# Layer 0 of a Mamba hybrid: two tiles' products in one instruction, both PSUM work tiles in one, and the carried state brought in by ScalarE

## The chip, the cores and the metric

The kernel runs on one core of one Trainium2 chip. The metric is the device time of one execution in microseconds; before the change the median of three runs is 3914.21 us. The profile is of one more execution. Engines are named as the profile names them: PE (matmuls), DVE (VectorE), ACT (ScalarE), POOL (GpSimd) and SP (whose queue issues the DMAs).

## The reference

The program is a chain of four layers on a (4, 96, 64, 64) image. The change touches layer 0 alone: two Mamba blocks in a row, each with a recurrence over the 4096 pixels.

```python
def _mamba_block(seq, ...):                       # seq: (4, 4096, 96)
    h = (seq - mu) * rsqrt(var + EPS) * ln_g + ln_b
    xs, z = split(h @ in_w, 2)                    # 192 channels each
    xc = silu(conv_b + sum(conv_w[:, k] * xp[:, k:k + L, :] for k in range(4)))
    dbl = xc @ xproj_w                            # dt (6), B (16), C (16)
    delta = softplus(dt @ dt_w + dt_b)
    dA = exp(delta[..., None] * A)                # 192 channels x 16 states
    dBx = delta[..., None] * Bm[:, :, None, :] * xc[..., None]
    # h[t] = dA[t] * h[t-1] + dBx[t]
    y = einsum('blds,bls->bld', hstates, Cm) + Dp * xc
    return (y * silu(z)) @ out_w
```

The recurrence has 4 x 192 x 16 independent rows of 4096 steps in each of the two blocks.

## The kernel before

**Items and tiles.** Layer 0 (`layer0`) splits the 4096 steps into four stretches of T = 1024. An *item* is one image, one stretch and one block: 32 items. An item has 24 *tiles* of 128 rows x 1024 steps: the 192 x 16 rows are cut by channel third p (0 to 2), state group g (0 to 3, four states each) and half j (0 or 1). `order` lists them; within a third it is the list `eight`. So there are 768 tiles, and the index `t` of a tile within its item runs from 0 to 23.

**What a tile needs.** DVE runs the recurrence (`tensor_tensor_scan`, L486): the decay `da`, the input `u`, a starting value from `state` (or 0 in the first stretch), and the states `hs` as output. ACT computes `da` = exp(delta x A) (L464). The input `u` is `udb` (delta times xc, repeated over four states) times B. For 8 of the 24 tiles (`pool_tiles`) POOL multiplies it from SBUF into `up` (L470), with B repeated by DMA into `brep`. For the other 16, PE repeats B into PSUM with a selection matrix (`rep`, L450: two matmuls in the program, four in the profile) and DVE multiplies (L482). POOL multiplies every `hs` with C (`crep`, L492), in place, and PE sums over the states into `y` (L511). ACT copies the last column of `hs` into `state` (L499).

**The PSUM work tiles.** Two tiles of 128 x 1024 fp32 lie in PSUM with one buffer each: tag `x` holds `rep`, tag `u` holds either a product `u` or, for the 8 tiles of POOL, their decay, then called `dap`. A product whose next tile is one of POOL's is written in place over `rep`.

**Order.** The engines' order is written out by hand in a loop over slots `m`, one tile per slot (`tc.manual_schedule`). Slot m issues the product and scan of tile m; then `dap` or `rep` of tile m + 1 (`rep` only at `group_starts`, since tiles with the same p and g share it); then `da` of tile m + 3 (`AHEAD`); then POOL's product with C of tile m - 1, the state copy of tile m - 3, and further back the sums over states, the gate with `z` (L522), the projection and the output. The first stage of a later item (norm, convolution, `dbl`, `delta`, `z`, and the DMAs that repeat rows over the partitions) is spread over the same slots by `at_slot`, whose number minus 24 is the slot relative to the item's first tile. Waits between engines are put in by the program's builder from the tiles that an instruction reads and writes; the author writes none.

Of the kernel before, what the change touches and what calls it, by code (L numbers as in the profile page):

```python
# [50 lines left out]
class Net:  # L51
# [43 lines left out]
    def layer0(self, dram, scratch):  # L95
        tc, nc, ins = self.tc, self.nc, self.ins
        x_in = ins["x"]
        with ExitStack() as ctx:
            cp = ctx.enter_context(tc.tile_pool(name="l0c", bufs=1))
            psum = ctx.enter_context(tc.tile_pool(name="l0p", bufs=2, space=PSUM))  # L100
            psum_x = ctx.enter_context(tc.tile_pool(name="l0x", bufs=1, space=PSUM))
            psum_y = ctx.enter_context(tc.tile_pool(name="l0y", bufs=2, space=PSUM))
# [11 lines left out]
            def wide(rows, cols, k):  # L114
                return psum_x.tile([128, T], F32, name="w_ps", tag="xu"[k % 2])[:rows, :cols]
# [113 lines left out]
            def global_pool():  # L229

                for b in range(B):
                    for s in range(NSC):
                        xt = wk.tile([128, T + 1], F32, name="gp_x", tag="hs", bufs=9)[:C, :T]
                        nc.sync.dma_start(xt, x_in[b, :, s * T : (s + 1) * T])
                        k = b * NSC + s
                        nc.vector.reduce_sum(pooled[:, k : k + 1], xt, axis=mybir.AxisListType.X)
                    yield
                pool4 = cp.tile([C, B], F32, name="pool4")
                nc.vector.reduce_sum(pool4, pooled.rearrange("p (b s) -> p b s", b=B), axis=mybir.AxisListType.X)
                ps = small(C, B)  # L240
                nc.tensor.matmul(ps, gpw, pool4, start=True, stop=True)
                gp = cp.tile([C, B], F32, name="gp")
                nc.scalar.activation(gp, ps, AF.Relu, scale=1.0 / L, bias=self.v("gp_b"))
                yield
                ps = small(C, B)
                nc.tensor.matmul(ps, fus[:, 1, :], gp, start=True, stop=True)
                nc.scalar.activation(fbias, ps, AF.Identity, bias=self.v("fus_b"))
                yield
# [6 lines left out]
            def first_stage(k):  # L255
# [11 lines left out]
                @at_slot(-11)  # L267
                def _():
                    m["xn"] = load_x(b, s, i) if k else x0


                @at_slot(-6)
                def _():
                    m["ps"] = [tile_ps(128), tile_ps(128)]
                    for q in range(8):
                        nc.tensor.matmul(
                            m["ps"][q // 4][:, q % 4 * C : q % 4 * C + C],
                            m["xn"][:, q * 128 : q * 128 + 128],
                            self.center,
                            start=True,  # L280
                            stop=True,
                        )

                @at_slot(-5)
                def _():
                    m["nt"] = cp.tile([128, 8, C], F32, name="nt", tag="nt")
# [11 lines left out]
                @at_slot(-4)  # L298
# [5 lines left out]
                @at_slot(-3)  # L304
# [7 lines left out]
                @at_slot(-2)  # L312
# [23 lines left out]
                parts_of("xc", [(w_x[:, i, k], k) for k in range(4)], n, ((-1, 1), (0, 2), (2, 4)), 2)  # L336

                @at_slot(4)
                def _():
                    nc.scalar.activation(m["xc"], m["xc"], AF.Silu)  # L340
                    exp_set()

# [3 lines left out]
                @at_slot(7)  # L346
# [4 lines left out]
                @at_slot(8)  # L351
# [6 lines left out]
                parts_of("delta", [(dtw[:, i], 0)], dbl, ((9, 10), (9, 10), (10, 11)), 1)  # L358

                @at_slot(11)  # L360
                def _():
                    nc.scalar.activation(m["delta"], m["delta"], AF.Softplus)  # L362
                    exp_set()

                parts_of("z", [(w_z[:, i], 3)], n, ((11, 12), (12, 13), (13, 14)), 3)

                @at_slot(12)
                def _():
                    m["dd"] = dram.tile([DIN, T], F32, name="dd", tag="dd", bufs=2)
                    for at, rows in both:  # L370
                        nc.sync.dma_start(m["dd"].rearrange("(p c) t -> c p t", p=3)[:, :, at], m["delta"][rows])

                def du(p):
                    if p == 0:
                        m["ud"] = dram.tile([DIN, T], F32, name="ud", tag="ud", bufs=2)
                    of = slice(p, p + 1)
                    u = wk.tile([128, 1, MB], F32, name="du", tag="du")
                    nc.gpsimd.tensor_mul(u, m["delta"][:, of], m["xc"][:, of])  # L378
                    to = m["ud"].rearrange("(p c) t -> c p t", p=3)[:, of]
                    for at, rows in both:  # L380
                        nc.sync.dma_start(to[:, :, at], u[rows])

                for p in range(3):
                    at_slot(14 + 3 * p)(lambda p=p: du(p))

                @at_slot(16)
                def _():
                    nc.scalar.activation(m["z"], m["z"], AF.Silu)
                    exp_set()


                for p in range(3):
                    for j in range(2):
                        at_slot((16, 24, 32)[p] + j)(lambda p=p, j=j: load_d(m, "dd", p, j))
                        at_slot((18, 26, 34)[p] + j)(lambda p=p, j=j: load_d(m, "ud", p, j))
                for g, t in ((0, 10), (1, 21), (3, 23), (2, 25)):
                    at_slot(t)(lambda g=g: load_c(m, g))
                at_slot(19)(lambda: load_b(m, 3))
                at_slot(15)(lambda: load_b(m, 2))
                return steps  # L400

# [9 lines left out]
            def load_c(made, g):  # L411
                made["crep", g] = load_s(made, "crep", NST + 4 * g, 5)
# [4 lines left out]
            def load_d(made, k, p, j):  # L417

                t = wk.tile([128, T], F32, name=f"{k}b", tag=f"{k}b", bufs=4)
                row = 64 * p + 32 * j  # L420
                for s4 in range(4):
                    nc.sync.dma_start(t[32 * s4 : 32 * s4 + 32], made[k][row : row + 32])
                made[k, p, j] = t
# [5 lines left out]
            eight = [(0, 0), (0, 1), (3, 0), (1, 1), (1, 0), (3, 1), (2, 0), (2, 1)]  # L429
            order = [(p, g, j) for p in range(3) for g, j in eight]  # L430
            pool_tiles = (2, 5, 7, 10, 13, 15, 18, 21)
            group_starts = (0, 3, 6, 8, 11, 14, 16, 19, 22)
            NTL = len(order)
# [9 lines left out]
            def rep(m):  # L443

                k, t = divmod(m, NTL)
                x = psum_x.tile([128, T], F32, name="rep", tag="x")
# [6 lines left out]
                return x  # L453

            def exp(m):
# [3 lines left out]
                if on_pool(m):  # L459
                    da = psum_x.tile([128, T], F32, name="dap", tag="u")  # L460
# [5 lines left out]
            def times_b(m):  # L466
                k, t = divmod(m, NTL)
                h, g, j = order[t]
                u = made[k]["u", t] = wk.tile([128, T], F32, name="up", tag="up", bufs=2)
                nc.gpsimd.tensor_mul(u, made[k]["ud", h, j], made[k]["brep", g])  # L470

            def scan(m, x):
# [4 lines left out]
                if on_pool(m):  # L477
                    u = made[k].pop(("u", t))
                else:

                    u = x if on_pool(m + 1) else psum_x.tile([128, T], F32, name="u", tag="u")
                    nc.vector.tensor_mul(u, made[k]["ud", h, j], x)  # L482
                hs = made[k]["hs", t] = wk.tile([128, T + 1], F32, name="hs", tag="hs", bufs=9)
                col = column(t)
                st = state[:, b, i, col : col + 1]
                nc.vector.tensor_tensor_scan(hs[:, 1:], made[k].pop(("da", t)), u, 0.0 if s == 0 else st, ALU.mult, ALU.add)  # L486

            def times_c(m):

                k, t = divmod(m, NTL)  # L490
                hs = made[k]["hs", t]
                nc.gpsimd.tensor_mul(hs[:, :T], hs[:, 1:], made[k]["crep", order[t][1]])  # L492

            def keep_state(m):
                k, t = divmod(m, NTL)
                b, s, i = items[k]
                col = column(t)
                if s < NSC - 1:
                    nc.scalar.copy(state[:, b, i, col : col + 1], made[k]["hs", t][:, T:])  # L499
# [5 lines left out]
            def sum_y(k, t0):  # L505

                for q, at in enumerate(halves):
                    for t in (t0, t0 + 1):
                        p, g, j = order[t]
# [4 lines left out]
                            made[k]["hs", t][:, at],  # L514
# [40 lines left out]
            b_slots = {2: 5, 4: 7, 7: 10, 9: 13, 12: 15, 15: 18, 18: 21, 23: NTL + 2}  # L555
# [3 lines left out]
            for m in sorted(stages[0])[:4]:  # L559
                for f in stages[0].pop(m):  # L560
                    f()
            prepare()
            wk = ctx.enter_context(tc.tile_pool(name="l0w", bufs=1))
            with tc.manual_schedule(engines=engines):
                gp = global_pool()
                first = min(stages[0])
                for m in range(first, last + 19):
                    k, t = divmod(m, NTL)
                    if 0 <= m < last:
                        scan(m, x)  # L570
                    if 0 <= m + 1 < last:
                        if on_pool(m + 1):
                            exp(m + 1)
                        elif (t + 1) % NTL in group_starts:
                            x = rep(m + 1)
                    if 0 <= m + AHEAD < last and not on_pool(m + AHEAD):
                        exp(m + AHEAD)
                    if 1 <= m <= last:
                        times_c(m - 1)
                    if 3 <= m < last + 3:  # L580
                        keep_state(m - 3)
                    if -1 <= m and t in b_slots and m - t + b_slots[t] < last:
                        times_b(m - t + b_slots[t])
                    for k0 in range(max(k - 1, 0), min(k + 1, len(items))):
                        at = m - NTL * k0
                        for p in range(3):
# [3 lines left out]
                            if at - 8 * p in (4, 6, 8, 10):  # L590
                                sum_y(k0, at - 4)
                            if at == 8 * p + 11:
                                gate(k0, p)
                        if at == 34:
                            made[k0]["x"] = load_x(*items[k0])
                        if at == 39:
                            project(k0)
                        if at == 41:
# [4 lines left out]
                    if m in (-20, -17, -14, -11, 15, 16):  # L603
# [878 lines left out]
```

## Time and profile before

| | |
|---|---|
| median of 3 runs | 3914.21 us (3908.41 to 3924.87) |
| the profiled execution's own time | 3925.66 us |
| its span, first to last instruction | 3923.9 us |
| mean granted PE clock | 0.855 |
| first and last scan of layer 0 start at | 77.34 and 2610.18 us |
| busy over the span | PE 82%, DVE 80%, ACT 62%, POOL 74% |
| DMA | 463.31 MB, mean 118 GB/s |

Layer 0 takes about two thirds of the span, and then come the other three layers. In the profile's groups a line reads: source line, engine, operation, output and inputs by the program's names, shapes, count; then busy time in all and mean ns of one; then the engine's idle time just before these instructions, and what ended most of it. In a timeline a line gives start and duration in us, and in square brackets the idle time before it with its releaser.

### The profile page before, as it was taken

How to read it: one execution, taken by the hardware profiler on the slowest of the kernel's cores; microseconds unless marked ns; L12 is line 12 of the kernel's file. 1: busy time of each engine (PE TensorE's matmuls, PEld its weight loads, DVE VectorE, ACT ScalarE, POOL GpSimd, SP SyncE). 2: the span in 40 equal slices, each digit the busy share in tenths (PEclk: the TensorE clock that was granted, in tenths of full speed). 3: DMA queues.
4: the chain of work that ended last, by engine and by line, in shares of the span. 5: the costliest groups of instructions: out<-in, count | busy, mean ns of one | idle time of the engine just before them, and what ended most of it. 6: DMA issues, size and time to landing. Idle time of an engine off the chain costs nothing. (4 is left out here: it accounts for less than half of the span.)

```text
span 3923.9 us, 43975 instructions
## 1 busy us (share of the span) xinstructions
PE 3205.9 (82%) x13534; PEld 1294.8 (33%) x13534; DVE 3154.4 (80%) x2772; ACT 2420.6 (62%) x4644; POOL 2911.4 (74%) x1443
## 2 busy tenths in 40 slices
PE   6887878877878788877878887755899988899988
PEld 3222222222222222222222222115644534666643
DVE  5999999999999999999999999973374385444649
ACT  4666667766766676666766666532254676666557
POOL 2999999999999999999999999961101064444427
PEclk7788878898788888888878878766899999999989
DMA  7567656675666566756676566636300000011101
GB/s 188 135 162 171 151 130 168 164 170 131 164 158 173 132 165 154 172 140 158 153 171 150 143 161 163 159 90 211 140 1 0 1 1 6 15 36 33 39 7 59
DMA packets 179828, 463.31 MB, mean 118 GB/s; under 512 B 52852, under 2 KB 54782, under 8 KB 176256
## 3 DMA queue, kind: packets, MB, share of 16 engines
q1 hardware_dynamic: 179592, 460.49, 46.7%
q8 instruction: 108, 1.77, 0.2%
q14 instruction: 128, 1.05, 0.1%
HBM read 386.81 MB, written 73.50 MB: 117 GB/s over the span
## 5 line engine op out<-in xcount | busy, mean ns | idle before, releaser
L492 POOL TENSOR_TENSOR hs<-hs,crep 128x1024 f32<-128x1024 f32 x768 | 1797.7, 2364 | 48.0 <-DVE hs L486 26.1
L450 PE MATMUL rep<-dbl,sel_b 32*128 32x512 f32 x1152 | 407.8, 785 | 495.8 <-DVE hs L486 428.3
L464 ACT ACTIVATE da<-ddb,nega 128x1024 f32<-128x1024 f32 x512 | 584.9, 1150 | 47.2 <-DVE hs L486 40.0
L470 POOL TENSOR_TENSOR up<-udb,brep 128x1024 f32<-128x1024 f32 x256 | 605.2, 2364 | 8.8 <-DMA brep<-cd 8.8
L464 ACT ACTIVATE dap<-ddb,nega 128x1024 f32<-128x1024 f32 x256 | 286.0, 1117 | 409.3 <-DVE hs L486 408.5
L511 PE MATMUL y<-hs,sel_r 128*32 128x512 f32 x3072 | 476.4, 690 | 5.5 <-POOL hs L492 5.5
L486 DVE TENSOR_TENSOR_SCAN hs<-da,state,rep 128x1024 f32<-128x1024 f32 x192 | 450.8, 2348 | 16.7
L486 DVE TENSOR_TENSOR_SCAN hs<-da,state,u 128x1024 f32<-128x1024 f32 x192 | 450.9, 2348 | 11.2 <-DVE u L482 1.4
L486 DVE TENSOR_TENSOR_SCAN hs<-dap,state,up 128x1024 f32<-128x1024 f32 x192 | 446.7, 2326 | 0.4 <-ACT dap L464 0.4
L210 PE MATMUL ps<-n,w_x 97*64 97x512 f32 x1536 | 408.0, 679 | 9.3 <-ACT n L319 6.6
L482 DVE TENSOR_TENSOR u<-udb,rep 128x1024 f32<-128x1024 f32 x256 | 314.7, 1229 | 74.4 <-PE rep L450 46.0
L450 PEld LDWEIGHTS rep<-dbl,sel_b 32*128 32x128 f32 x1152 | 107.0, 214 | 794.5 <-issue 595.7
L482 DVE TENSOR_TENSOR rep<-udb,rep 128x1024 f32<-128x1024 f32 x256 | 310.3, 1212 | 0.2
L1040 POOL CAST hq<-y 128x1536 fp8e5<-128x1536 f16 x64 | 94.0, 1469 | 219.3 <-issue 122.6
L210 PEld LDWEIGHTS ps<-n,w_x 97*64 97x64 f32 x1536 | 118.6, 153 | 295.2 <-issue 243.5
L511 PEld LDWEIGHTS y<-hs,sel_r 128*32 128x32 f32 x3072 | 65.2, 114 | 336.5 <-issue 208.5
L378 POOL TENSOR_TENSOR du<-delta,xc 128x512 f32<-128x512 f32 x96 | 122.6, 1277 | 64.7 <-ACT delta L362 50.2
L914 POOL MEMSET h<- 1x4096 f32 x1 | 3.5, 3507 | 212.8 <-DVE n L820 212.8
L1179 POOL TENSOR_TENSOR av<-av,ec 128x780 f32<-128x780 f32 x32 | 58.8, 1837 | 133.2 <-ACT av L1176 133.2
L486 DVE TENSOR_TENSOR_SCAN hs<-da,rep 128x1024 f32<-128x1024 f32 x64 | 146.5, 2289 | 5.4
L224 PE MATMUL ps<-xc,xproj 64*102 64x512 f32 x384 | 147.3, 924 | 3.5 <-ACT xc L340 3.5
L486 DVE TENSOR_TENSOR_SCAN hs<-da,u 128x1024 f32<-128x1024 f32 x64 | 146.4, 2288 | 3.7 <-DVE u L482 0.5
(262 smaller groups left out, 6137.7 us busy)
## 6 DMA issues: line engine op xcount, KB each, us to landing
ddb<-dd SPq DMA_DIRECT2D x768, 128.0 KB
udb<-ud SPq DMA_DIRECT2D x768, 128.0 KB
crep<-cd SPq DMA_DIRECT2D x512, 128.0 KB
brep<-cd SPq DMA_DIRECT2D x256, 128.0 KB
dd<-delta SPq DMA_DIRECT2D x64, 384.0 KB
ud<-du SPq DMA_DIRECT2D x192, 128.0 KB
band<-in_band SPq DMA_DIRECT2D x24, 1024.0 KB
x<-in_x SPq DMA_DIRECT2D x32, 384.0 KB
```

Of the source, the lines that this page charges most:

```text
L210: nc.tensor.matmul(ps[rows], w[:, 64 * p : 64 * p + 64], rhs[:, at.start + shift : at.stop + shift], start=k == 0, stop=k == len(ws) - 1, ...
L224: nc.tensor.matmul(ps, w[rows, p], x[rows, p], start=start and p == 0, stop=p == 2)
L378: nc.gpsimd.tensor_mul(u, m["delta"][:, of], m["xc"][:, of])
L450: nc.tensor.matmul(x[:, at], sel_b[rows, order[t][1]], made[k]["dbl"][rows, at], start=True, stop=True)
L464: nc.scalar.activation(da, made[k]["dd", h, j], AF.Exp, scale=nega[:, col : col + 1])
L470: nc.gpsimd.tensor_mul(u, made[k]["ud", h, j], made[k]["brep", g])
L482: nc.vector.tensor_mul(u, made[k]["ud", h, j], x)
L486: nc.vector.tensor_tensor_scan(hs[:, 1:], made[k].pop(("da", t)), u, 0.0 if s == 0 else st, ALU.mult, ALU.add)
L492: nc.gpsimd.tensor_mul(hs[:, :T], hs[:, 1:], made[k]["crep", order[t][1]])
L511: nc.tensor.matmul(made[k]["y", p][row : row + 32], sel_r, made[k]["hs", t][:, at], start=False, stop=True, skip_group_check=True,)
L1040: nc.gpsimd.tensor_copy(q, y2, saturate=False)
L1179: nc.gpsimd.tensor_add(v[:, 2:4], v[:, 0:2], ec)
```

## The change

One PSUM tile `pair_ps` of 128 x 2 x 1024 takes the place of tags `x` and `u`: half 1 holds what `rep` held, half 0 what `u` and `dap` held. Its halves are used by the same instructions as the two tiles were, with these differences:

- Where two neighbouring tiles with the same p and g are both DVE's (`paired`, 6 of an item), one product of 2048 columns reads half 1 twice and writes both halves; `order` has two tiles exchanged so that they are neighbours. Four products of 1024 columns stay.
- `hs` holds both j of a pair (5 buffers of 2 x 1025 in place of 9 of 1025). POOL multiplies both with C in one instruction of 2 x 1024 columns, and the state copy takes two columns. POOL's products with B of group 3 are paired too, and `du` becomes one product of 1536 columns in place over `delta`.
- For the 16 tiles of DVE the scan starts from the constant 1.0 (0.0 in the first stretch), and ACT multiplies the first column of `da` with the state (`enter`). The 8 tiles of POOL read the state as before.
- `udb` is loaded by pairs, `crep` has one buffer per group, `nt` shares a buffer with `up2`, the Silu of `z` stands behind that of `xc`, and the first stage's slots and the slots of gate, projection and output move.

The diff, cut to its core:

```diff
+            pair_ps = psum_x.tile([128, 2, T], F32, name="pair")
...
-                parts_of("xc", [(w_x[:, i, k], k) for k in range(4)], n, ((-1, 1), (0, 2), (2, 4)), 2)
+                parts_of("xc", [(w_x[:, i, k], k) for k in range(4)], n, ((-3, -1), (-2, 0), (0, 2)), 2)
...
+                    nc.gpsimd.tensor_mul(m["delta"], m["delta"], m["xc"])
+                    spread_out("delta", "ud")
...
             def load_c(made, g):
-                made["crep", g] = load_s(made, "crep", NST + 4 * g, 5)
+                made["crep", g] = load_s(made, f"crep{g}", NST + 4 * g, 1)
...
-            eight = [(0, 0), (0, 1), (3, 0), (1, 1), (1, 0), (3, 1), (2, 0), (2, 1)]
+            eight = [(0, 0), (0, 1), (3, 0), (1, 0), (1, 1), (3, 1), (2, 0), (2, 1)]
...
+            paired = (0, 3, 8, 11, 16, 19)
+            ends = {1: 0, 4: 1, 5: 3, 7: 2}
...
             def rep(m):
...
-                x = psum_x.tile([128, T], F32, name="rep", tag="x")
+                x = pair_ps[:, 1]
...
                 if on_pool(m):
-                    da = psum_x.tile([128, T], F32, name="dap", tag="u")
+                    da = pair_ps[:, 0]
...
+            def enter(m):
+                k, t = divmod(m, NTL)
+                b, s, i = items[k]
+                col = column(t)
+                if s:
+                    a0 = made[k]["da", t][:, :1]
+                    nc.scalar.mul(a0, a0, state[:, b, i, col : col + 1])
+
+            def twice(x):
+                return x[:, None, :].to_broadcast([128, 2, T])
...
                 if on_pool(m):
-                    u = made[k].pop(("u", t))
+                    u = made[k].pop(("up", h, g, j))
+                elif t in paired:
+                    u = pair_ps[:, 0]
+                    nc.vector.tensor_mul(pair_ps, made[k]["ud", h], twice(pair_ps[:, 1]))
+                elif t - 1 in paired:
+                    u = pair_ps[:, 1]
                 else:
-
-                    u = x if on_pool(m + 1) else psum_x.tile([128, T], F32, name="u", tag="u")
-                    nc.vector.tensor_mul(u, made[k]["ud", h, j], x)
-                hs = made[k]["hs", t] = wk.tile([128, T + 1], F32, name="hs", tag="hs", bufs=9)
+                    u = pair_ps[:, 1 if on_pool(m + 1) else 0]
+                    nc.vector.tensor_mul(u, made[k]["ud", h][:, j], pair_ps[:, 1])
+                if ("hs", h, g) not in made[k]:
+                    made[k]["hs", h, g] = wk.tile([128, 2, T + 1], F32, name="hs", tag="hs", bufs=5)
+                hs = made[k]["hs", h, g][:, j]
...
-                nc.vector.tensor_tensor_scan(hs[:, 1:], made[k].pop(("da", t)), u, 0.0 if s == 0 else st, ALU.mult, ALU.add)
+                nc.vector.tensor_tensor_scan(hs[:, 1:], made[k].pop(("da", t)), u, 0.0 if s == 0 else st if on_pool(m) else 1.0, ALU.mult, ALU.add)
...
+            def times_c(k, p, g):
+
+                hs = made[k]["hs", p, g]
+                nc.gpsimd.tensor_mul(hs[:, :, :T], hs[:, :, 1:], twice(made[k]["crep", g]))
```

## The prediction

> **What bounds the kernel now.** I read the page's first two parts first, then the busy time of the stretch that the change touches.
>
> ```profile
> PE 3205.9 (82%) x13534; PEld 1294.8 (33%) x13534; DVE 3154.4 (80%) x2772; ACT 2420.6 (62%) x4644; POOL 2911.4 (74%) x1443
> ...
> DVE  5999999999999999999999999973374385444649
> ...
> POOL 2999999999999999999999999961101064444427
> PEclk7788878898788888888878878766899999999989
> ```
>
> The first 26 of the 40 slices are layer 0, and there VectorE (DVE) and GpSimd (POOL) are both at nine tenths. The busy time of each engine from 75 to 2612 us says it more finely (columns: PE, PEld, DVE, ACT, POOL, granted clock, DMA share, GB/s):
>
> ```profile
> 75.00:2612.00 2537.00, 2026.70 (x8230) 582.10 (x8230) 2431.20 (x1378) 1650.79 (x3004) 2484.72 (x1122) 0.82 0.63 154
> ```
>
> POOL is busy 98% of it and DVE 96%: two engines bind together. The DVE timeline has the first scan at 77.34 us and the last at 2610.18: 2532.8 us for 767 tiles, so 79.2 us for an item of 24 tiles, 32 items in all. The groups give the durations:
>
> ```profile
> L492 POOL TENSOR_TENSOR hs<-hs,crep 128x1024 f32<-128x1024 f32 x768 | 1797.7, 2364 | 48.0 <-DVE hs L486 26.1
> L450 PE MATMUL rep<-dbl,sel_b 32*128 32x512 f32 x1152 | 407.8, 785 | 495.8 <-DVE hs L486 428.3
> ...
> L464 ACT ACTIVATE dap<-ddb,nega 128x1024 f32<-128x1024 f32 x256 | 286.0, 1117 | 409.3 <-DVE hs L486 408.5
> ...
> L486 DVE TENSOR_TENSOR_SCAN hs<-da,state,u 128x1024 f32<-128x1024 f32 x192 | 450.9, 2348 | 11.2 <-DVE u L482 1.4
> L486 DVE TENSOR_TENSOR_SCAN hs<-dap,state,up 128x1024 f32<-128x1024 f32 x192 | 446.7, 2326 | 0.4 <-ACT dap L464 0.4
> ...
> L482 DVE TENSOR_TENSOR u<-udb,rep 128x1024 f32<-128x1024 f32 x256 | 314.7, 1229 | 74.4 <-PE rep L450 46.0
> ...
> L486 DVE TENSOR_TENSOR_SCAN hs<-da,rep 128x1024 f32<-128x1024 f32 x64 | 146.5, 2289 | 5.4
> ```
>
> The last column matters most. PE and ACT wait long for scans (428 us before `rep`, 408 us before `dap`), yet DVE waits 0.4 us for `dap` and 46 us for `rep`: both are made while DVE does something else. The timeline shows with what (start, duration, idle before in brackets; DVE, then ACT, then PE):
>
> ```profile
> 1265.58 2.35 DVE L486 TENSOR_TENSOR_SCAN hs<-da,state,u 128x1024 f32<-128x1024 f32 x1
> 1267.84 1.21 DVE L482 TENSOR_TENSOR rep<-udb,rep 128x1024 f32<-128x1024 f32 x1
> 1269.15 2.35 DVE L486 TENSOR_TENSOR_SCAN hs<-da,state,rep 128x1024 f32<-128x1024 f32 x1
> 1271.41 2.33 DVE L486 TENSOR_TENSOR_SCAN hs<-dap,state,up 128x1024 f32<-128x1024 f32 x1
> 1273.94 1.23 DVE L482 TENSOR_TENSOR u<-udb,rep 128x1024 f32<-128x1024 f32 x1 [0.20 <-PE rep L450]
> ```
> ```profile
> 1267.96 1.12 ACT L464 ACTIVATE dap<-ddb,nega 128x1024 f32<-128x1024 f32 x1 [6.26 <-DVE hs L486]
> ```
> ```profile
> 1254.62 2.07 PE L450 MATMUL rep<-dbl,sel_b 32*128 32x512 f32 x4 [3.14 <-DVE hs L486]
> ...
> 1272.76 1.13 PE L450 MATMUL rep<-dbl,sel_b 32*128 32x512 f32 x4
> ```
>
> Tiles 0, 1, 2 of an item: `dap` for tile 2 starts when scan 0 has freed `u` (1267.93) and is ready at 1269.08, under product 1 and scan 1, 2.3 us before scan 2. `rep` for tile 3 lies under scan 2. That works because `rep` and `u`/`dap` are two tiles in PSUM, and each waits only for the readers of its own.
>
> [...]
>
> **The change, part by part, per item.** Start-to-start times are read off the DVE timeline.
>
> Removed from DVE: six products become halves of six others. Two now take 1.26 + 1.31. One of 2048 columns takes 1.26 and 1024 columns more, [...]1.13 by the trace (1229 less the 665 of the 512-column gate, doubled)[...]. Sixteen scans get the constant 1.0 in place of a state column, 2289 against 2348: 16 x 0.06 = 1.0 us (24 of 32 items; the others had a constant). [...] Added to ACT: 16 multiplies of one column, near the 0.19 us of a state copy, 0 to 3 us; removed: 12 state copies (2.2) and one pair of table loads (2.6). ACT is busy 1650.8/32 = 51.6 of 79 us, so either sign is hidden. Moved at no cost, with one answer: the steps of `nt`, `xc`, `dbl`, `delta` and `z`, two to four slots earlier or later, and on SP the loads (as many as before: 24 + 24 of `ddb`, `udb`, 16 + 8 of `crep`, `brep` per item; `ud` in two stores instead of six). Each keeps three slots or more before its use, and a slot grows to 4.3 us below. `crep` has one buffer per group, so its load waits for POOL's last product of that group, up to five slots before the next use. `delta` times `xc`, now in place, holds POOL until the `dd` stores have landed; the cover is POOL's slack, 75 busy of over 100 us. If that cover were gone, a landing of some us per item would be DVE's too.
>
> Moved, and this decides: both PSUM tiles are now one, `pair_ps`. In the built program each wait can be followed to the instruction that raises its semaphore. Before, `dap` of tile 2 waits for scan 0, and `rep` of tile 3 for scan 1. After, `dap` of tile 2 waits for scan **1**, and `rep` of tile 3 for scan **2**, although they touch the other half: a write waits for the last reader of any part of the tile. All eight `dap` and all nine `rep` of an item wait this way for the scan just ahead of their user on DVE. So nothing covers them:
>
> - `dap`: 0.03 (scan end to ACT start, in 132 cases) + 1.12 + 0.10 (132.82 to 132.92, one of DVE's four waits for it) = 1.24 us, with a ready ACT. x8 = 9.9. Bounds 1.2 to 1.5. Behind it on ACT wait `da` and the state copies, three tiles ahead, so not urgent.
> - `rep`: 0.14 + matmuls + 0.05. Matmuls are 1.13 warm, 2.08 cold, 1.49 on average where PE had waited. PE will wait more; I take half and half, 1.60: 1.79 us. x9 = 16.1. Bounds 1.32 and 2.27.
> - `rep` of tile 0 also queues on PE behind 32 `w_x` matmuls (0.27 us each) and one y sum (1.07), 9.6 us, moved between it and `rep` of tile 22; DVE offers 1.26 + 2.2 + 1.33 + 2.3 = 7.1. Late by 2.5, colder 4.7, warmer 1.3; I take 3.0.
>
> The DVE chain itself: products 6 x 2.36 + 5.1 for four singles = 19.3; DVE scans 6 x 2.20 + 10 x 2.29 = 36.1 (a scan that ends a stretch counts whole); POOL-fed scans 8 x 2.33 = 18.6; the three gates fall into `rep` waits. 74.0. With 9.9 + 16.1 + 3.0 it is **103.0 us per item**, against 79.2: +23.8, x32 = **+762 us**. The profiled run's own time is 3925.7 (span 3923.9 and 1.8 around it), 11.5 over the median 3914.2; the difference is added to the median: **4676 us**.
>
> **Rivals.**
>
> *PE cold throughout.* PE's 2026.7/32 = 63.3 us of work at clock 0.82 would be 104 at 0.5, as long as the item. `rep` 2.27 x 9 = 20.4, lateness 4.7: 109.0, +954, 4868. For it: the stretch after layer 0, 57% busy, has clock 0.61. Against: more backlog is more activity.
>
> *PE warm.* 1.32 x 9 = 11.9, lateness 1.3: 97.1, +573, 4487.
>
> *The other side: the waits are covered.* If ACT and PE found their half free as before, what remains is the saving: Start to start, DVE needs 20.7 for products, 55.5 for scans and 1.8 for gates, 77.9 in all (parts rounded), and POOL 32 x 2.31 + 3 x 1.23 = 77.6; less 2.3 and 2.6 that is 75.6 and 75.0, and with the 1.3 lost today an item takes about 77.0: 32 x -2.2 = -70, 3844. The point of decision: the 17 waits may cost 2.2 us together, 0.13 each. One exponential alone is 1.12 with scans directly ahead and behind, so this needs the written waits not to bind. That the change doesn't do what it says is excluded: six products of 2048 columns and sixteen multiplies of one column stand in the built program for each item.
>
> **How the numbers follow.** Mixed clock 0.62, cold 0.16, warm or some waits shorter 0.13, waits covered 0.05, no net effect 0.02, worse than cold 0.02. The range goes from a little below the warm case to a little over the cold one: 4470 to 4890. Changes below 0.5% (some 20 us) can't be told from none. Faster 0.05, same 0.02, slower 0.93.
>
> **What would show it.** Right: DVE idle before POOL-fed scans, released by ACT, near 256 x 1.2 = 310 us; DVE idle before products, released by PE, 500 to 600 us; DVE at seven tenths, POOL likewise, in layer 0; the 2048-column product near 2.3 us, scans with the constant near 2.29. Wrong: DVE still at nine tenths, or `dap` starting while the scan ahead of its user still runs. If POOL or the DMA queues release DVE's waits, a buffer is the cause that I costed at nothing.

## The result, and the profile after

The changed kernel takes **4769.59 us** (median of four runs, 4759.98 to 4773.55) against 3916.86 for the kernel before: a ratio of 1.217, interval 1.214 to 1.221. The forecast was 4676, range 4470 to 4890.

First the page's first two parts, of the kernel after: busy time of each engine, then the slices of DVE, POOL and the granted PE clock.

```profile
PE 3453.8 (72%) x13534; PEld 1316.8 (28%) x13534; DVE 3126.9 (66%) x2580; ACT 2390.5 (50%) x4678; POOL 2704.7 (57%) x899
...
DVE  3777777777777777777777777777633726644548
...
POOL 1767666676676666667666666766610003554427
PEclk7677777776777777677777767767668999999999
```

DVE and POOL do no more work than before (3126.9 us against 3154.4, and 2704.7 against 2911.4), yet both have gone from nine tenths to seven. PE has as many matmuls as before, and takes 3453.8 us for them instead of 3205.9. What layer 0 has gained is waits, not work. The busy time from 110 to 3395 us, with the columns as before, shows the clock as well: 0.72, where it was 0.82.

```profile
110.00:3395.00 3285.00, 2226.99 (x8070) 594.53 (x8068) 2356.99 (x1163) 1605.10 (x3008) 2237.71 (x571) 0.72 0.47 117
```

The groups of the page say who waits for whom in their last column:

```profile
L461 PE MATMUL pair<-dbl,sel_b 32*128 32x512 f32 x1152 | 520.5, 995 | 1082.1 <-DVE hs L519 1076.8
...
L474 ACT ACTIVATE pair<-ddb,nega 128x1024 f32<-128x1024 f32 x256 | 286.2, 1118 | 1216.2 <-DVE hs L519 1172.3
...
L508 DVE TENSOR_TENSOR pair<-udb,pair 128x2048 f32<-128x2048 f32 x192 | 440.8, 2296 | 434.2 <-PE pair L461 432.0
L519 DVE TENSOR_TENSOR_SCAN hs<-pair,state,up 128x1024 f32<-128x1024 f32 x192 | 451.3, 2351 | 243.0 <-ACT pair L474 243.0
...
L513 DVE TENSOR_TENSOR pair<-udb,pair 128x1024 f32<-128x1024 f32 x128 | 157.3, 1229 | 172.6 <-PE pair L461 171.5
L519 DVE TENSOR_TENSOR_SCAN hs<-pair,up 128x1024 f32<-128x1024 f32 x64 | 146.6, 2291 | 80.7 <-ACT pair L474 80.7
```

Before, DVE waited 0.4 us for `dap` and 46 us for `rep`. Now it waits 323.7 us (243.0 + 80.7) for `dap` and 603.5 (432.0 + 171.5) for `rep`; and PE and ACT, over 1,000 us each, wait for scans. Each side waits for the other in turn. The DVE timeline shows a round of it:

```profile
1511.75 2.35 DVE L519 TENSOR_TENSOR_SCAN hs<-pair,state,up 128x1024 f32<-128x1024 f32 x1 [1.19 <-ACT pair L474]
1516.28 2.30 DVE L508 TENSOR_TENSOR pair<-udb,pair 128x2048 f32<-128x2048 f32 x1 [2.18 <-PE pair L461]
1518.71 4.46 DVE L519 TENSOR_TENSOR_SCAN hs<-da,pair 128x1024 f32<-128x1024 f32 x2
1524.42 2.35 DVE L519 TENSOR_TENSOR_SCAN hs<-pair,state,up 128x1024 f32<-128x1024 f32 x1 [1.25 <-ACT pair L474]
```

The scan of a POOL tile stops 1.2 us for its decay; after it the product stops 2.18 us for `rep`. The decay starts 0.04 us after the end of the scan just ahead (a pair of scans merged in one line, which ended at 1510.56):

```profile
1510.60 1.12 ACT L474 ACTIVATE pair<-ddb,nega 128x1024 f32<-128x1024 f32 x1 [2.70 <-DVE hs L519]
```

And the PE timeline of the same stretch shows why the other wait is 2.18:

```profile
1514.16 2.08 PE L461 MATMUL pair<-dbl,sel_b 32*128 32x512 f32 x4 [4.53 <-DVE hs L519]
...
1527.14 1.06 PE L541 MATMUL y<-hs,sel_r 128*32 128x512 f32 x8
1528.14 1.13 PE L461 MATMUL pair<-dbl,sel_b 32*128 32x512 f32 x4
```

`rep` starts 0.06 us after the scan ends at 1514.10, and after 4.53 us of idleness takes 2.08 us, at a granted clock of 0.50 (1514.10 to 1516.30 us). The one at 1528.14, behind other matmuls, takes 1.13, at 1.00 (1528.15 to 1529.25). These two are what cold and warm mean here and in the prediction; the kernel before has the same two clocks around its `rep`s of 2.07 us (1254.60 to 1256.70: 0.50) and of 1.13 (1272.76 to 1273.90: 1.00).

So it is everywhere in the layer. In the kernel before, all 256 `dap` and 273 of 287 `rep` (the very first has no scan ahead of it) start before the end of the scan just ahead of their user. In the kernel after, none of either does: 254 `dap` and 248 `rep` start within 0.1 us after that end, the others later.

The time is in three places. Before layer 0's first scan: 108.91 us instead of 77.34, +31.6. Between first and last scan (at 3451.42): 3342.5 us for 767 tiles, **104.6 us an item** instead of 79.2, +809.7. After it: +6.7. Together 848, the difference of the two spans (4771.8 and 3923.9).

### The profile page after: what moved, and what is told of

It is laid out like the page before. It is cut to its first block, busy times and chain, and to the rows that moved or that the text cites. A ratio compares the mean times of both kernels' runs of the same rounds, so it can differ in the third digit from the quotient of the medians.

```text
span 4771.8 us, 42439 instructions
## 1 busy us (share of the span) xinstructions
PE 3453.8 (72%) x13534; PEld 1316.8 (28%) x13534; DVE 3126.9 (66%) x2580; ACT 2390.5 (50%) x4678; POOL 2704.7 (57%) x899
## 5 line engine op out<-in xcount | busy, mean ns | idle before, releaser
L524 POOL TENSOR_TENSOR hs<-hs,crep 128x2048 f32<-128x2048 f32 x384 | 1597.3, 4171 | 1079.1 <-DVE hs L519 810.0
L461 PE MATMUL pair<-dbl,sel_b 32*128 32x512 f32 x1152 | 520.5, 995 | 1082.1 <-DVE hs L519 1076.8
L519 DVE TENSOR_TENSOR_SCAN hs<-da,pair 128x1024 f32<-128x1024 f32 x512 | 1150.2, 2278 | 37.4 <-ACT state L530 0.5
L474 ACT ACTIVATE pair<-ddb,nega 128x1024 f32<-128x1024 f32 x256 | 286.2, 1118 | 1216.2 <-DVE hs L519 1172.3
L508 DVE TENSOR_TENSOR pair<-udb,pair 128x2048 f32<-128x2048 f32 x192 | 440.8, 2296 | 434.2 <-PE pair L461 432.0
L519 DVE TENSOR_TENSOR_SCAN hs<-pair,state,up 128x1024 f32<-128x1024 f32 x192 | 451.3, 2351 | 243.0 <-ACT pair L474 243.0
L474 ACT ACTIVATE da<-ddb,nega 128x1024 f32<-128x1024 f32 x512 | 584.3, 1143 | 19.1 <-DMA ddb<-dd 14.3
L494 POOL TENSOR_TENSOR up<-udb,brep 128x2048 f32<-128x2048 f32 x96 | 434.9, 4530 | 23.9 <-DMA crep<-cd 23.1
L513 DVE TENSOR_TENSOR pair<-udb,pair 128x1024 f32<-128x1024 f32 x128 | 157.3, 1229 | 172.6 <-PE pair L461 171.5
L519 DVE TENSOR_TENSOR_SCAN hs<-pair,up 128x1024 f32<-128x1024 f32 x64 | 146.6, 2291 | 80.7 <-ACT pair L474 80.7
L534 PE MATMUL y<-xc,dp 128*128 128x512 f32 x192 | 164.1, 951 | 0.0
L497 POOL TENSOR_TENSOR up<-udb,brep 128x1024 f32<-128x1024 f32 x64 | 150.4, 2351 | 0.0
L386 POOL TENSOR_TENSOR delta<-delta,xc 128x1536 f32<-128x1536 f32 x32 | 110.1, 3439 | 67.7 <-DMA dd<-delta 66.6
```

The lines of the kernel that those rows point to most:

```text
L461: nc.tensor.matmul(x[:, at], sel_b[rows, order[t][1]], made[k]["dbl"][rows, at], start=True, stop=True)
L474: nc.scalar.activation(da, made[k]["dd", h, j], AF.Exp, scale=nega[:, col : col + 1])
L494: nc.gpsimd.tensor_mul(up, u, twice(made[k]["brep", 3]))
L497: nc.gpsimd.tensor_mul(up, u[:, 1], made[k]["brep", g])
L508: nc.vector.tensor_mul(pair_ps, made[k]["ud", h], twice(pair_ps[:, 1]))
L513: nc.vector.tensor_mul(u, made[k]["ud", h][:, j], pair_ps[:, 1])
```

## The experiments

Each is compared with runs of the kernel before on the same chip, which were between 3914 and 3921 us at the median.

**1. The joined tile alone, in the kernel before.** Nothing else of the change.

```diff
+            both_ps = psum_x.tile([128, 2, T], F32, name="both")
...
-                x = psum_x.tile([128, T], F32, name="rep", tag="x")
+                x = both_ps[:, 1]
...
-                    da = psum_x.tile([128, T], F32, name="dap", tag="u")
+                    da = both_ps[:, 0]
...
-                    u = x if on_pool(m + 1) else psum_x.tile([128, T], F32, name="u", tag="u")
+                    u = both_ps[:, 1 if on_pool(m + 1) else 0]
```

> The kernel before, with one edit: its two PSUM work tiles become the two halves of one tile; no product is paired, nothing else moves. Theory (a write waits for the last reader of any part of the tile): DVE work 78 us per item less 1.8 of gates that fall into waits, 8 waits for dap of 1.27 and 9 for rep of about 2.0 give 104 to 107 us per item against 79.2, so 4710 to 4800 us in all, with DVE idle before POOL-fed scans near 310 us and before products over 500. Rival (the longer POOL and DVE instructions, the fewer hs buffers or the moved first stage cost the time): 3900 to 3950 us, since none of these is in this kernel.

Measured: 4811.52 us, ratio 1.230 (1.226 to 1.234), a little over the range expected, an item at 106.9 us. The waits are there as well:

```profile
L483 DVE TENSOR_TENSOR both<-udb,both 128x1024 f32<-128x1024 f32 x512 | 628.4, 1227 | 573.4 <-PE both L451 492.2
...
L487 DVE TENSOR_TENSOR_SCAN hs<-both,state,up 128x1024 f32<-128x1024 f32 x192 | 451.4, 2351 | 261.7 <-ACT both L465 211.2
```

With the scans of the first stretch (86.0), DVE is idle 348 us before the scans of POOL's tiles. This one edit costs more than the whole change. With the joined tile given, the rest of the change saves 2.3 us an item (106.9 to 104.6) and loses time at the start.

**2. Two tiles again, in the kernel after.** All else stays, except that the six products of 2048 columns must be twelve single ones.

```diff
-            pair_ps = psum_x.tile([128, 2, T], F32, name="pair")
...
-                x = pair_ps[:, 1]
+                x = rep_ps["x"] = psum_x.tile([128, T], F32, name="rep", tag="x")
...
-                    da = pair_ps[:, 0]
+                    da = psum_x.tile([128, T], F32, name="dap", tag="u")
...
```

> The changed kernel with the two PSUM tiles apart again, so its six paired DVE products are twelve single ones again; POOL's pairs, the multiply on ScalarE and all moved steps stay. Theory: the waits go back to the scan before last; DVE needs 76.9 and POOL 75.0 us per item, with 1.3 lost 78.2, so 32 x -1.0 = -32 against the kernel before, and +38 for the start and the end as in the changed kernel: 3880 to 3960 us. Rival (pairs on POOL, hs buffers or moved steps cost the time): over 4500 us.

Measured: 3941.08 us, ratio 1.007 (1.005 to 1.010), as the theory has it. DVE's waits for PE from 130 to 2600 us:

```profile
DVE u L508 <- PE rep L461: 28.6, 30, 6.5
DVE rep L508 <- PE rep L461: 24.2, 12, 3.2
```

53 us instead of some 600, and none for `dap`. An item takes 78.8 us, 0.4 less than before; what is left of the loss is the start (first scan at 106.66). Runs 1 and 2 together settle the cause: the joined tile brings the loss by itself (run 1 has no paired product), and without it the loss between the first and the last scan is gone.

**3. Only `dap` out of the joined tile.** The decays of POOL's tiles go to SBUF, three tiles ahead like the others; pairs and joined tile stay.

```diff
-                if on_pool(m):
-                    da = pair_ps[:, 0]
-                else:
-                    da = wk.tile([128, T], F32, name="da", tag="da", bufs=AHEAD + 1)
+                da = wk.tile([128, T], F32, name="da", tag="da", bufs=AHEAD + 1)
...
```

> The changed kernel with the decay of POOL's eight tiles written to SBUF, in the da buffers and three tiles ahead like the others; the joined PSUM tile and the six paired products stay. Theory: no wait for dap is left, and since a POOL-fed scan no longer reads PSUM, rep waits for the scan before it and is made under it in 8 of 9 cases; only rep of tile 0 stays exposed (2 to 3 us). 75.7 + 1.3 + 2.5 = 79.5 us per item, 3920 to 4020 us with the start as in the changed kernel. Rival (dap alone costs, rep is late because PE is slow): only the 8 x 1.27 us go, about 4450 us. Rival (a scan with both inputs in SBUF is slowed by POOL): POOL-fed scans over 2.6 us, 4050 us or more.

Measured: 4320.18 us, ratio 1.104 (1.102 to 1.107): a miss for the theory on time; the second rival came true. The waits did go (none for `dap`, 100.4 us for `rep`), but two groups of this run's page show what came instead:

```profile
L521 POOL TENSOR_TENSOR hs<-hs,crep 128x2048 f32<-128x2048 f32 x384 | 1966.1, 5148 | 141.7 <-DMA crep<-cd 112.6
...
L516 DVE TENSOR_TENSOR_SCAN hs<-da,state,up 128x1024 f32<-128x1024 f32 x192 | 742.5, 3867 | 0.0
```

The scan with both inputs in SBUF takes 3867 ns on average instead of 2351, POOL's product with C 5148 instead of 4171. The spread (minimum / median / maximum in ns) says how:

```profile
L516 DVE TENSOR_TENSOR_SCAN hs<-da,state,up x192: 2323/3902/6539, 839.3 to 2995.2; 128x1024 f32<-128x1024 f32 x192
```

The fastest such scan is as fast as ever, 2323 ns; the slowest is longer by 4216, about as long as one POOL product with C (median 4224). What either waits for inside is not shown; that both lengthened, with the decays in SBUF, is. Per item the scans give back (64 x 1.62 + 192 x 1.52)/32 = 12.4 us. This is what holding `dap` in PSUM avoids.

**4. Only `enter`, in the kernel before.** ACT multiplies the first decay of the 16 DVE tiles with the state, the scans start from 1.0.

```diff
+            def enter(m):
+                ...
+                    nc.scalar.mul(a0, a0, state[:, b, i, col : col + 1])
-u, 0.0 if s == 0 else st, ALU.mult, ALU.add)
+u, 0.0 if s == 0 else st if on_pool(m) else 1.0, ALU.mult, ALU.add)
```

> The kernel before with ScalarE's multiply for the 16 DVE tiles and the constant 1.0 in their scans; nothing else. Theory: 16 x 0.06 us less on DVE in 24 of 32 items, but POOL, with 77.6 us per item, binds beside DVE: 0 to -23 us, I expect -8. Rival (ScalarE's 16 extra instructions delay the exponentials): slower by 10 to 60 us, with DVE waiting for da.

Measured: 3907.32 us, ratio 0.999 (0.9975 to 1.000), scans at 2289 ns. A gain of some 7 us, at the edge of what can be told from none.

**5. The start: one memset off POOL, in the kernel after.**

```diff
-                        nc.gpsimd.memset(n[:, :3], 0.0)
+                        nc.vector.memset(n[:, :3], 0.0)
```

In the kernel after, POOL's timeline at the start is this (start, duration, idle before):

```profile
90.45 4.49 POOL L494 TENSOR_TENSOR up<-udb,brep 128x2048 f32<-128x2048 f32 x1 [23.12 <-DMA crep<-cd]
94.88 0.10 POOL L320 MEMSET n<- 97x3 f32 x1
```

and PE's, which waits for that memset and then does 32 matmuls ahead of the first `rep`:

```profile
95.04 10.37 PE L211 MATMUL ps<-n,w_x 97*64 97x512 f32 x32 [25.07 <-POOL n L320]
105.34 1.13 PE L461 MATMUL pair<-dbl,sel_b 32*128 32x512 f32 x4
```

> The changed kernel with one instruction moved: the three zero columns of n are set by DVE and not by POOL. In the trace of the changed kernel that memset stands behind POOL's first product with B (at 90.45, after 23.12 us of waiting for a DMA), the 32 matmuls with w_x of the next item wait 25.07 us for it, and the first rep stands behind those on PE. Theory: this alone is the late start; the first scan comes at 78 to 86 us instead of 108.9, and the time falls by 23 to 31 us, to 4738 to 4747. Rival: PE or DVE would have waited for the same DMA anyway; then the first scan stays after 100 us and the time within 10 us of 4770.

Measured: 4759.24 us (ratio 1.2145, 1.212 to 1.217), 10 less than the kernel after, with intervals that overlap; the first scan comes at 91.50, 17.4 earlier. Half of the theory. The view of waits puts the 10.93 us for which DVE then stands idle down to a DMA, but two things end together there. The first product starts at 89.10 and the first `rep` ends at 89.06: it still stands behind the 32 matmuls (from 78.33), and these behind the memset, which on DVE comes at 78.11, after sums over the input of which one waited 15.01 us for its load. The eight loads of `udb` land almost as late, at 87.8 at the latest: they are issued from 79.64 us on, against 69.97 in the kernel before. A reason for that is that the product of `delta` and `xc` on POOL is one piece, in place, and waits for the `dd` stores. Both are read off the trace, not tried.

**6. PE kept busy, in the kernel after.** Added matmuls against a column of zeros, ahead of every `rep`:

```diff
...
+                            for _ in range(10):
+                                nc.tensor.matmul(
+                                    made[ks]["y", ps][:32], sel_r, zero_w[:, :1].to_broadcast([128, MB]),
+                                    start=False, stop=True, skip_group_check=True,
+                                )
```

> The changed kernel with ten more matmuls on PE ahead of each rep (sel_r against a column of zeros, added to y, so nothing changes in y). PE then works while it waits for the scan, some 2.7 us warm or 5.2 us cold, instead of standing idle for about 4.5 us. Theory: rep costs 2.08 us instead of 1.13 because PE had been idle; kept busy it runs at the full clock, the mean rep matmul falls from 995 to below 800 ns, each of the nine rep waits of an item by 0.5 to 0.9 us, and the time by 150 to 260 us, to 4510 to 4620. Rival: the granted clock is low for another reason (the chip limits PE whatever it does); then rep stays at 995 ns or more, the added matmuls take their cold 5.2 us and some of them still run when the scan ends, and the time is 4770 to 5000.

Measured: 5523.15 us, ratio 1.410 (1.407 to 1.413), beyond both expectations, because the added matmuls took 0.88 us each and not 0.27: ten of them outlast the wait. (I had sized them by the sums over states, whose eight records take 1.06 us, and the cold 5.2 us of ten by a quarter of the 2.08 us of a cold `rep`. The sums write four different groups of 32 rows, the added ones all the same; that this is the reason wasn't tried.) For the clock it decides: granted 0.978 over the execution, where the kernel after has 0.775, and the mean `rep` matmul takes 641 ns instead of 995, so that a `rep` takes 1.13 us. The low clock of the kernel after is thus no limit that holds whatever PE does. The same with four, and none ahead of the `rep` of tile 0:

> The changed kernel with four added matmuls (sel_r against a column of zeros, added to y, which they leave as it is) ahead of eight of the nine reps of an item, none ahead of the rep of tile 0. In the run with ten ahead of all nine each took 0.88 us, PE was 99% busy, its clock 0.98 and every rep 1.13 us, but the added matmuls themselves outlasted the scans. Four take 3.5 us, less than the 4.5 to 6 us that PE stands idle before a rep in the changed kernel. Theory: rep is cold because PE stood idle; with 1 to 2 us of idleness left it stays near the full clock, DVE's wait before a product falls from about 2.18 to 1.25 us, 0.9 x 8 x 32 = 230 us less at best, time 4530 to 4660. Rival: an idle stretch of 1 to 2 us already costs the clock, or the added work makes as many reps late as it speeds up: time 4740 or more.

Measured: **4600.27 us**, ratio 1.174 (1.171 to 1.177), as the theory has it: more work on PE, a granted clock of 0.927, and 169 us less. PE's groups and DVE's waits of this run:

```profile
L464 PE MATMUL pair<-dbl,sel_b 32*128 32x512 f32 x1152 | 360.1, 704 | 474.4 <-DVE hs L522 473.2
```
```profile
DVE hs L522 <- ACT pair L477: 323.0, 256, 1.7
DVE pair L511 <- PE pair L464: 282.8, 191, 25.9
DVE pair L516 <- PE pair L464: 158.6, 95, 3.4
```

The waits for `rep` fall from 603.5 to 441.4 us, by 162; those for `dap` stay.

**7. Without `dap`, in the kernel after.**

```diff
-                nc.scalar.activation(da, made[k]["dd", h, j], AF.Exp, scale=nega[:, col : col + 1])
+                if not on_pool(m):
+                    nc.scalar.activation(da, made[k]["dd", h, j], AF.Exp, scale=nega[:, col : col + 1])
```

> The changed kernel without the exponentials of POOL's eight tiles (dap): their decay is whatever half 0 of the pair tile holds, so this leaves a third of the decays out of the computation. Theory: the eight waits are simply serial with DVE, 8 x 1.24 x 32 = 317 us (the profile has 323.6 us of DVE waiting for ACT); they go, nothing takes their place, and the time is 4430 to 4470. The waits for rep stay, since its half's tile is still read by the scan just ahead. Rival: part of them covers something else (PE's queue ahead of rep, POOL's products), so that DVE waits there instead; then the gain is under 250 us, time above 4520.

Measured: 4369.12 us, ratio 1.115 (1.113 to 1.117), 400 less than the kernel after and below the theory's range. The 324 us of waits are gone and nothing took their place. Beyond that the waits for `rep`, without the one at the start, fell from 579.3 to 538.9, since PE now idles less before a `rep` (745.1 us in all instead of 1082.1; its mean matmul is 903 ns instead of 995). The two waits feed each other, which the theory left out. Some 30 us more come of the scans of POOL's tiles, which now follow another scan directly: they start 2.18 us after its start, and it is 2.26 long.

**8. A version that beats both.** Run 2 left POOL 90% busy and DVE 95%: larger POOL products had bought slack on the engine that no longer bound. So one more product per item (tile 23) goes from DVE to POOL, with two PSUM tiles and the memset of run 5.

```diff
-            pool_tiles = (2, 5, 7, 10, 13, 15, 18, 21)
+            pool_tiles = (2, 5, 7, 10, 13, 15, 18, 21, 23)
...
-            b_slots = {..., 20: (1, 0, 3)}
+            b_slots = {..., 20: (1, 0, 3), 21: (0, 2, 2)}
...
-                at_slot(15)(lambda: load_b(m, 2))
+                at_slot(22)(lambda: load_b(m, 2))
```

> The changed kernel with two separate PSUM tiles again (twelve single products), the memset of n on DVE, and one more tile of each item, the 24th, given to POOL's product with B (nine instead of eight). In the run with separate tiles POOL was busy 2250.7 us of 2490 (90%) and DVE 2365.6 (95%), an item taking 78.8 us. Theory: DVE binds and POOL has slack; a product of 1.2 us leaves DVE, 2.35 us go to POOL (72 to 74.5 us of work per item), the item falls to 77.4 to 77.8 us, and with the start 25 us earlier the time is 3862 to 3890, below the kernel before. Rival: POOL at 74.5 us is so near the item that every late DMA of B or C is DVE's too (it waited 143 us for DMAs in that run); then an item takes 79 us or more and the time is 3915 or above.

Measured: 3915.89 us, ratio 0.9996 (0.9988 to 1.0005), no difference; an item at 78.5 us. The rival's time, though not its reason: DVE waits 66.0 us in 31 items for the ninth product itself (2.1 each, not the 0.9 of the next expectation), which stands behind a 4.5 us product for the next item. So the two change places:

```diff
+            b_slots = {..., 20: (0, 2, 2), 21: (1, 0, 3)}
```

> The kernel with two PSUM tiles and nine POOL tiles again, POOL's product for the ninth (tile 23) issued one slot earlier, ahead of the paired product of 4.5 us for the next item and not behind it. In the run before, DVE waited 66.0 us for that product (0.9 us in 31 items, and 0.76 for the rep behind it), an item taking 78.5 us. Theory: the ninth product comes 4.2 us earlier, those waits go, an item takes 76.6 to 77.2 us and the time is 3855 to 3880, below the kernel before. Rival: POOL, with 73.6 us of work per item, then makes another scan wait (the next item's paired product is now later by 2.4 us); time 3900 to 3925.

Measured: 3899.31 us, ratio 0.996 (0.994 to 0.998), above the theory. The wait for POOL is gone, but 88.2 us of waits for `rep` stand in its place: 62.6 for tile 0, whose `rep` queues on PE behind 32 `w_x` matmuls (7.1 us), and 25.6 for tile 14, which the next expectation lays to tile 0 too. So half of those matmuls move behind the `rep` of tile 0:

```diff
-((-3, -1), (-2, 0), (0, 2))
+((-3, -1), (-1, 1) if k else (-2, 0), (0, 2))
```

> The run with nine POOL tiles, the ninth early, and one more move: of the 32 w_x matmuls (7.1 us) that stand on PE ahead of the rep of tile 0, half are issued one slot later, behind that rep. In the run before, that rep started 9.07 us after the rep of tile 22 although its tile had been free sooner, and DVE waited 62.6 + 25.6 us for PE, nearly all of it there; apart from those waits DVE had nothing to wait for. Theory: the rep of tile 0 comes 3.6 us earlier, the waits fall from 88 to under 35 us, an item from 78.2 to 76.6 to 77.2 us, and the time from 3899 to 3845 to 3870. Rival: the silu of xc, which waits for the last of these matmuls on ACT, makes dap of tile 2 or 5 late instead, or POOL (73.6 us an item) binds; then 3890 or more.

Measured: **3853.87 us**, ratio 0.983 (0.981 to 0.986), time and item as expected: 67 us below the kernel before on the same chip (3920.92), or 1.7%. DVE's waits from 130 to 2560 us, and the busy time from 130 to 2500:

```profile
DVE rep L508 <- PE rep L461: 40.8, 13, 3.3
DVE u L508 <- PE rep L461: 7.3, 6, 1.7
```
```profile
130.00:2500.00 2370.00, 1935.48 (x7978) 561.61 (x7979) 2265.37 (x1304) 1574.29 (x2954) 2268.41 (x587) 0.82 0.64 161
```

The waits are 48.1 us and not under 35: those for tile 0 fell from 62.6 to 7.3 us, but those for tile 14 (the first line) rose from 25.6 to 40.8. DVE and POOL are level, 2265 and 2268 us of 2370, and an item takes 76.9 us. Whether another queue order alone would help the kernel before, whose DVE waited 46 us for `rep`, was not tried.

## Why the prediction was right, and where it was off

**The joined tile decides, by waits for the scan just ahead: right.** Runs 1 and 2 show it from both sides. The rival on the other side, covered waits, would have needed `dap` and `rep` to start during that scan; none did, all 256 scans of POOL's tiles in the kernel after waited for ACT, and 286 of the 288 products that follow a `rep` for PE.

**The wait for `dap`, 8 x 1.24 = 9.9 us an item: right.** 323.7 us over 256 waits is 1.26 each, 10.1 an item, and run 7 shows that they were all on the path.

**The wait for `rep`, 9 x 1.79: too low by the clock.** The step "half and half, 1.60" for the matmuls failed. Of 217 `rep`s between 130 and 2650 us whose four matmuls the timeline shows together, 67% take over 1.9 us, 24% under 1.2, and the mean is 1.80. The argument against the cold rival, that more backlog is more activity, points the wrong way: a PE that waits idles mostly 4 to 6 us right before `rep` (101 of the 217).

**The rep of tile 0, 3.0 us late: too high.** It does start 2.5 us late, as the sum 9.6 less 7.1 says, but then takes 1.16 us: behind other matmuls, it is warm. From the end of the scan just ahead to its product 3.75 us pass, not 1.79 + 3.0, which is 1.0 less than forecast. For the eight others it is 2.04 on average, 2.0 more in all. That the two errors partly cancel is luck: 19.1 us forecast for `rep` in all, of which 1.8 under the gates; measured 603.5 less 24.2 at the start, over 32, is 18.1 plus the gates' 1.8, so 19.9.

**The DVE chain, 74.0 us: near.** 104.6 less 10.1 less 19.9 is 74.6. The 2048-column product is 2.30 us long, as forecast, but 2.43 from start to start (1516.28 to 1518.71), not 2.36: 0.4 of the 0.6. Both forecasts were the author's estimates: 1.26 and the 1.13 that the trace gives for 1024 columns more make 2.39 from start to start. The sum for an item was thus 103.0 against 104.6. Of the 94 us that the forecast was short this is 48 (809.7 less 762); the start and the end, below, are 38, and the remaining 8 come of setting the medians beside two profiled executions that lie 11.5 and 4.0 us over theirs.

**Moved steps at no cost: right in the steady state, wrong at the start.** Once scans pace the slots, POOL's waits for stores cost nothing (run 2: 78.8 us an item, though POOL waited 143 us for DMAs; in the kernel after `delta` times `xc`, L386, waited 66.6 us for the `dd` stores, start included, 2.1 an item). Ahead of the first scan nothing hides them, and 31.6 us were lost there, 6.7 more after the last scan. The forecast used the argument "three slots or more before its use" where the slots have no scans in them yet.

**The savings.** The constant's 0.06 us per scan was right in duration (2348 to 2289), but worth only 7 us in run 4, where POOL, busy 2486.1 of the 2525 us from 75 to 2600, binds together with DVE. Taken with all other parts, run 2 saves 0.4 us an item. The rival with covered waits gave an item 77.0 us and assumed that both savings reach the end: 2.3 us on DVE, of which the constant is 1.0 and the paired products 1.3, and 2.6 us on POOL. The 1.3 and the 2.6 were the author's estimates. Estimated from the trace alone they are 6 x 0.18 = 1.1, with the 2.39 above, and 17 instructions fewer on POOL x 0.19 = 3.2 (2 x 1277 less 2364 ns, `du` and the product with C in the kernel before). Run 2, with covered waits but without the 1.3 us of the paired products, takes 78.8, so about 0.5 us an item of the savings did not arrive.

## What to carry to other kernels

Before two buffers are made one, so that an instruction can span them, list who waits for whom on each: where the waits go by the whole buffer, a producer that ran one instruction ahead now runs behind the last reader of either half, and its full duration lands on the path. A wait that was added to PE cost more here than its matmuls did before, because after the idleness ahead of them they ran cold (2.08 us instead of 1.13); price it at the cold time. And when a change makes an engine faster that isn't alone at the bound, look for work to hand to it: with a ninth tile on POOL, one memset moved and the queue order mended twice, the kernel with two tiles went from 3941 to 3854 us, 67 below the kernel before, while the faster instructions by themselves were worth little (0.4 us an item in run 2).

## What the runs showed of the hardware

- `rep` against PE's idle time just ahead of it, in the kernel after from 130 to 2650 us: none or up to 2 us, 1.13 us in all 47 cases; 2 to 3 us, 1.68 on average (20 cases); over 3 us, 2.03 (150 cases). Added work of no use on PE (run 6, four matmuls) raised the granted clock from 0.775 to 0.927 and shortened the kernel by 169 us.
- With the decay of POOL's tiles in SBUF (run 3), the scans that read decay, state and input from SBUF took 2323 to 6539 ns, with a median of 3902, and POOL's product with C 4147 to 6216. With the decay in PSUM, the same scans beside the same products of POOL take 2323 to 2353 (run 2 and the kernel after).
- POOL's product of 2 x 1024 columns with C takes 4171 ns and two of 1024 took 2 x 2364 = 4728: 0.56 us less. The product with B, of 2048 columns, takes 4530, 0.20 less. The one with C is in place and reads C twice; which of the two makes it faster no run shows, but at 1024 columns, in place or not, both products took 2364.
